# A decoder layer on one core: a new order of the steady slot on all engines

## The chip, the cores and the metric

The kernel runs on one core of a Trainium2 chip. The metric is the device time of one execution in microseconds (us). Five engines work side by side: PE (TensorE, matrix products and transposes), DVE (VectorE), ACT (ScalarE), POOL (GpSimd) and SP (SyncE, which issues most of the transfers). Each engine works through its own list of instructions in order, and they wait for each other by semaphores.

## The reference

The inputs are 16 sequences of 128 tokens with 256 features, and a context of the same shape. All arithmetic is in float32. Cut to what matters:

```python
x = x + self_attention(layernorm(x))                  # 16 heads of 64, no mask
x = x + cross_attention(layernorm(x), context, mask)  # 16 heads of 16, masked keys
x = x + experts(layernorm(x))                         # 8 experts of 512, all are evaluated

# experts: top-1 gate g -> norm_g = g / (g + 1e-6)
h = gelu(einsum('nd,edh->neh', xf, w1) + b1)
y = einsum('neh,ehd->ned', h, w2) + b2
out = (y * norm_g[:, None, None]).sum(axis=1)
```

Because the gate's factor does not depend on the expert, the experts can be summed before they are scaled. The change does not touch the expert stage.

## The kernel before

**Slots.** The two attentions run as a software pipeline of 16 slots, one for each sequence. Slot s does the self attention of sequence s, the first half of the cross attention of sequence s - 1 (queries, scores, softmax) and the second half of the cross attention of sequence s - 2 (transposed probabilities, values, output). It also does the key, query and value projections of two coming sequences at a time, by a Strassen-like scheme of seven products in place of eight. Slots 2 to 13 have nearly the same content and are called steady here. After slot 15 comes a short drain, and then the experts (from about 500 us on).

**The order is a table.** Every step of a slot is pushed on a heap by `at(name, f)` with a due time: slot s starts at `EXTRA + s * SLOT`, and `DUE[name]` is added. `run_slots` then pops all steps in order of these times and emits their instructions. PE, DVE, ACT and POOL are scheduled manually, so this order is the order of each engine's list. `FIRST_DUE` and `SECOND_DUE` hold exceptions for slots 0 and 1. A due time above `SLOT` reaches into the next slot. The due times set the order alone: what starts when is decided on the chip by the semaphores.

**The steps that matter here**, by the names in the table:

- `S0`, `S1`: self scores of one half of the heads each (`self_scores`, L693). `max0`, `max1`: largest score (L394, DVE). `ex0a` to `ex1b`: four exponentials each (L400, ACT). `r0a` to `r1b`: reciprocals of the sums (L411, DVE). `mul0a` to `mul1b`: normalization (L415, POOL). `T1a1` to `T1b2`: four transposes each (L430, PE), evacuated from PSUM by `T1a1e` to `T1b2e` on ACT.
- The same with a `c` or as `T2...` for the cross attention: `CQ` queries (L806), `q2T` their evacuation on DVE, `CS` scores (L828), `msk0`, `msk1` the mask, `cmax`, `cex`, `cr`, `cmul`, then `T2a1` to `T2b2`, of which `T2a1e`, `T2a2e` run on ACT and `T2b1e`, `T2b2e` on DVE.
- `SVa`, `SVb`: self values (L718), evacuated by `atT0`, `atT1` on DVE. `CV`: cross values (L867), `at2T`. `SO`, `CO`: output projections (L738, L887), added to the tokens by `xsSO`, `xsCO`.
- `cvr`: cross value rows (L782, `cross_value_rows`), evacuated by `cvre` on ACT. `ck`: cross keys (L755, `cross_keys`), evacuated by `cke`, `cke2` on ACT.
- `bn`, `bn3`, `root`, `xn`, `xn3`: statistics, inverse root (12 small DVE instructions) and normalization. `ab1`, `ab2`: a bias added to the tokens on POOL (L383). `LNx`, `LN1`, `LN3`: transposes of normalized tokens (L379), evacuated by `LNxc`, `LN1c`, `LN3c` on ACT.
- The paired projections: `v1x`, `v1y`, `v2x`, `v2y` for values (L643), and the same with q and k for queries and keys (L552). The first step opens one PSUM tile with the halves a and b, the second one with f and e; the third adds to a, the fourth to f and e. `vu0` to `vu3`, `vc00`, `vc1`, `vc0` read the halves out (and the same with q and k): `u1` reads b, `c00` reads a for the last time, `c1` and `c0` read f and e for the last time.

**Narrow steps.** The score and value products use a part of the array: `S0`, `S1` in row tiles of 64, `CS` in row tiles of 32, `CV` in column tiles of 32, `SVa`, `SVb` in column tiles of 64. All others use the whole array.

**PSUM.** The scores have a pool of two tiles of two banks each. All other outputs of PE share `ps_mm`, four tiles of one bank each:

```python
ps_mm = both.enter_context(
    tc.tile_pool(name="ps_mm", bufs=4, space=bass.MemoryType.PSUM, side="right")
)
```

**Transfers.** The context of two sequences is one load, double buffered; the load for the group after next is issued by SP behind the last use of the present one. In slots 14 and 15 the first two quarters of `w1` are loaded (`load_w1`, at `S0`), and `pre_hidden` starts on expert products at the places that the projections leave free (`PRE_STEPS`).

Of the kernel before, what the change touches and what calls it, by code (L numbers as in the profile page):

```python
# [30 lines left out]
GB = 2  # L31
NG = B // GB
# [17 lines left out]
NROW = 528  # L50


SLOT = 26.98
EXTRA = 7.86
DUE = dict(
    S0=0.0, S1=1.0, T2a1=2.05, T2a2=2.49, T2a1e=2.69, ck=2.92, T2a2e=3.19, max0=3.47, v1x=3.79,
    cke=3.99, vu0=4.3, cke2=4.4, max1=4.61, v1y=4.66, q1x=5.52, ex0a=5.54, vu1=6.08, q1y=6.42,
    vu2=6.76, qu0=6.91, vu3=7.24, r0a=7.32, v2x=7.32, mul0a=7.39, vc00=7.4, ex0b=7.41, qu1=7.63,
    v2y=7.77, qu2=8.06, qu3=8.49, LNx=8.6, q2x=8.64, vc1=8.84, q2y=9.09, LNxc=9.1, ex1a=9.13,
    vc0=9.19, r0b=9.53, mul0b=9.81, qc1=10.19, cvr=10.21, qc00=10.51, qc0=10.54, r1a=10.98,  # L60
    T2b1=11.23, mul1a=11.26, cvre=11.31, ex1b=11.66, T2b2=11.66, T2b1e=11.86, CQ=12.1,
    T2b2e=12.46, T1a1=12.97, q2T=13.17, T1a2=13.4, r1b=13.51, xn1=13.6, T1a1e=13.6, mul1b=13.79,
    CS=13.93, st0=14.0, mid=14.0, late=14.0, T1a2e=14.1, ab1=14.9, CV=14.97, msk0=15.08,
    LN3=16.07, at2T=16.27, T1b1=16.29, LN3c=16.49, msk1=16.61, T1b2=16.73, T1b1e=16.93,
    LN1=17.16, T1b2e=17.43, SVa=17.47, cmax0=17.8, LN1c=17.93, SVb=18.38, tf=18.93, mid2=18.93,
    atT0=18.94, late2=18.94, cex0a=19.12, k1x=19.43, atT1=19.54, cmax1=20.14, k1y=20.33,
    cex0b=20.49, SO=21.23, cr0a=21.28, cmul0a=21.56, ku0=21.86, cr0b=22.14, cex1a=22.36,
    cmul0b=22.58, ku1=22.58, ku2=23.01, ku3=23.44, cex1b=23.74, cr1a=23.94, st1=24.0,
    cmul1a=24.3, k2x=24.68, xsSO=24.88, k2y=25.12, bn=25.28, kc00=25.32, cr1b=25.78, CO=26.03,
    cmul1b=26.06, kc1=26.22, kc0=26.57, xsCO=27.09, bn3=27.5, root=28.09, xn=34.27, ab2=34.3,  # L70
    xn3=37.78,
)


FIRST_DUE = dict(
    fk0=-11.4, fq0=-9.5, fk0e=-9.4, fq0e=-7.7, fk1=-7.2, norm1=-7.0, S0=-5.4, fk1e=-5.3,
    fq1=-4.4, max0=-4.0, cross=-3.0, ex0a=-2.7, fLN=-2.65, fq1e=-2.6, fv0=-2.3, fLNc=-1.4,
    r0a=-1.32, ex0b=-1.3, mul0a=-1.2, S1=-0.6, fv0e=0.1, r0b=0.15, mul0b=0.2, fab0=0.25,
    fab1=0.3, max1=0.4, fv1=0.41, ex1a=1.65, early0=1.7, early1=1.75, cvr=2.22, fv1e=3.0,
    r1a=3.1, mul1a=3.2, early2=3.3, early3=3.35, ex1b=3.6, q0=3.96, cvre=5.0, r1b=5.1,  # L80
    mul1b=5.2, q0e=5.3, early=5.4, k0=6.57, ke0=8.56, ws0=8.7, v0=9.18, xn1=10.44, T1a1=10.9,
    ve0=11.1, T1a2=11.34, T1a1e=11.54, T1b1=11.77, T1a2e=12.14, T1b2=12.21, LN1=12.64,
    T1b1e=12.74, LN1c=13.06, T1b2e=13.34, w0q=13.6, w0k=13.7, SVa=14.25, SVb=15.15, atT0=15.42,
    q1=17.2, atT1=17.21, wv0=17.3, q1e=17.6, k1=18.0, w1q=18.1, tf=18.2, SO=19.16, ke1=19.6,
    ws1=19.7, w1k=20.0, xsSO=22.81, bn=23.22, v1=23.47, root=24.79, xn=25.0, ck=25.2, ve1=25.39,
    q1x=26.9, cke=26.9, cke2=26.91, qu0=26.95, q1y=27.8, qu1=28.2, ab2=28.44, ab1=28.5,
    k1x=28.7, qu2=28.8, k1y=28.9, qu3=29.2, ku0=29.3, ku1=29.85, ku2=30.0, ku3=30.1, q2x=30.5,
    q2y=30.95, qc00=31.0, qc1=32.0, qc0=32.5, k2x=32.8, kc00=33.3, k2y=33.4, kc1=34.5, kc0=34.9,
# [15 lines left out]
def decoder_layer(  # L104
# [53 lines left out]
    def psum_mm(name):  # L158
        return ps_mm.tile([P, 512], F32, tag="mm", name=name)
# [51 lines left out]
    def context(g):  # L211
        c = work.tile([P, KD, GT], F32, tag="ctx", name=f"ctx{g}")
        nc.sync.dma_start(out=c, in_=ctxT[g])
        return c

    contexts = {0: context(0)}
# [55 lines left out]
    def urgent():  # L272

        return tc.high_priority()
# [5 lines left out]
    def at(name, f, *a):  # L280


        if now[0] is None:
            f(*a)
        else:
            heapq.heappush(events, (when(name), next(count), now[0], f, a))

    def due(name, f, *a):

        if now[0] is None:  # L290
            with urgent():
                f(*a)
        else:
            at(name, f, *a)

    def when(name):
# [3 lines left out]
        if s == 1 and name in SECOND_DUE:  # L300
            return EXTRA + SLOT + SECOND_DUE[name]
        return EXTRA + s * SLOT + DUE[name]

# [445 lines left out]
    def cross_keys(b):  # L749
        kT = work.tile([P, C2, 2, T], F32, tag="k2T", name="k2T")  # L750
        g, i = b // GB, b % GB
        mm = psum_mm("mm_k2")[:, : C2 * T].rearrange("p (m t) -> p m t", m=C2)
        for m in range(C2):
            for k in range(KD):
                nc.tensor.matmul(  # L755
                    mm[:, m, :],
                    wx[:, 1, k, m * P : (m + 1) * P],
                    contexts[g][:, k, i * T : (i + 1) * T],
                    start=(k == 0),
                    stop=(k == KD - 1),  # L760
                )


        def out(m):
            for e in range(2):
                nc.scalar.activation(
                    kT[:, m, e, :],
                    mm[:, m, :],
                    AF.Identity,
                    bias=bkp[:, e, m : m + 1],  # L770
                    scale=par[:, e : e + 1],
                )

        due("cke", out, 0)
        due("cke2", out, 1)
        entry["k2T", b] = kT

    def cross_value_rows(b):
        g, i = b // GB, b % GB
        mm = psum_mm("mm_v2")  # L780
        for k in range(KD):
            nc.tensor.matmul(  # L782
                mm[:, :D],
                contexts[g][:, k, i * T : (i + 1) * T],
                wx_vo[:, 0, k, :],
                start=(k == 0),
                stop=(k == KD - 1),
            )
        due(
            "cvre",  # L790
            nc.scalar.copy,
            v2s[g % 2][:, i].rearrange("p (e w) -> p e w", e=2)[:, :, :D].rearrange(
                "p e (r t) -> p e r t", t=32
            )[:, :, :, :DH2],
            mm[:, :D].rearrange("p (r e d) -> p e r d", e=2, d=DH2),
        )
        if i == GB - 1 and g + 2 < NG:
            contexts[g + 2] = context(g + 2)

    def cross_queries(b):  # L800
        xnT2 = entry.pop(("xnT2", b))
# [210 lines left out]
    def slot(s):  # L1012


        for half in range(2):
            at(f"S{half}", self_scores, s, half)
            at(f"SV{'ab'[half]}", self_values, s, half)
            for n in range(2):
                at(f"T1{'ab'[half]}{n + 1}", self_transposed, s, half, n)
                if s >= 2:  # L1020
                    at(f"T2{'ab'[half]}{n + 1}", cross_transposed, s - 2, half, n)
        at("SO", self_output, s)
        at("cvr", cross_value_rows, s)
        at("ck", cross_keys, s)
        normalize_outputs(s, s - 2 if s >= 2 else None)
        if s >= 1:
            at("LNx", cross_norm, s - 1)
            at("CQ", cross_queries, s - 1)
            at("CS", cross_scores, s - 1)
            at("CS", cross_softmax, s - 1)  # L1030
        if s >= 2:
            at("CV", cross_values, s - 2)
            at("CO", cross_output, s - 2)
        if s >= 3:
            at("LN3", expert_norm, s - 3)
        bs = [2, 3] if s == 0 else [s + 3, s + 4] if s % 2 and s + 4 < B else []
# [3 lines left out]
        if bs:  # L1040
            at("LN1", self_norm_transposed, bs)
        b0 = s + 2 - s % 2
# [18 lines left out]
        if s >= B - 2:  # L1061
            at("S0", load_w1, s - (B - 2), we1)
        for n, (s1, name, out) in enumerate(PRE_STEPS):
# [459 lines left out]
```

## Time and profile before

| | |
|---|---|
| median of 3 runs | 858.39 us (858.09 to 858.63) |
| the profiled execution | 858.56 us |
| its span | 856.8 us |
| PE busy | 846.4 us (99%) |
| PE weight loads busy | 721.0 us (84%) |
| DVE busy | 642.6 us (75%) |
| ACT busy | 473.7 us (55%) |
| POOL busy | 164.1 us (19%) |
| granted TensorE clock | 0.999 |

The busy time of an engine is the union of its instructions' times. PE's instructions overlap: each starts before the one ahead of it has ended, so small stops do not show in the busy share but in the distance between starts. In the timeline rows of the profile the columns are the start in us, the length in us, engine, line, operation, output and inputs, the tile of the array and the shape, and the count of instructions merged into the row. In the rows of waits the columns are total us, times and longest us.

### The profile page before, as it was taken

To read this page: it belongs to the slowest core of one execution; us is meant where nothing else is said; L and a number is where in the kernel's file an instruction comes from. 1 tells how busy PE (TensorE), PEld (TensorE's weight loads), DVE (VectorE), ACT (ScalarE), POOL (GpSimd) and SP (SyncE) were. 2 spreads that over 40 slices of the span, in tenths; PEclk is the share of its full clock that TensorE was granted. 3 is DMA by queue.
4 is the path that set the end of the run, shared out by engine and by line. 5 is a ranking of instruction groups with operands and counts; after the bars stand their busy time and mean duration, and the time that the engine had idled before them with its cause. 6 is when DMAs were issued, how large, how long until landed. Compare 5 with 4: busy or idle time off the path is not lost.

```text
span 856.8 us, 16387 instructions
## 1 busy us (share of the span) xinstructions
PE 846.4 (99%) x5934; PEld 721.0 (84%) x5934; DVE 642.6 (75%) x1697; ACT 473.7 (55%) x1720; POOL 164.1 (19%) x179
## 2 busy tenths in 40 slices
PE   9999999999999999999999999999999999999997
PEld 7899889898898988898765458888888888888886
DVE  5888998989888888888657497776566756576655
ACT  3567677776877768686774523343434343343332
POOL 5133242432424334232341000000000000000000
PEclk9999999999999999999999999999999999999999
DMA  8500000000000000001240100000000000000000
GB/s 238 148 14 2 2 15 1 14 1 2 14 1 14 2 2 14 2 1 50 93 170 34 50 1 0 1 13 13 1 0 1 26 1 0 1 13 13 2 0 26
DMA packets 18321, 21.32 MB, mean 25 GB/s; under 512 B 9584, under 2 KB 13696, under 8 KB 17600
## 3 DMA queue, kind: packets, MB, share of 16 engines
q1 hardware_dynamic: 17728, 19.93, 7.4%
q8 instruction: 47, 0.77, 0.4%
q0 software_dynamic: 368, 0.30, 0.2%
q14 instruction: 34, 0.28, 0.1%
q10 hardware_dynamic: 144, 0.04, 0.0%
HBM read 18.16 MB, written 2.10 MB: 24 GB/s over the span
## 4 chain that ended last, share of the span: by engine, by line
PE 90%; DVE 6%; ACT 2%; issue 1%; DMA 1%; DVEq 0%; SPq 0%
PE y L1264 19%; PE mm_qk L552 10%; PE mm_o L738 6%; PE tr_p L430 6%; PE he L1264 5%; PE hf L1264 5%; PE ha L1264 5%; PE mm_v L643 5%; PE sc L693 4%; PE po L718 3%; PE mm_h L1002 3%; PE hb L1264 3%; PE po L867 2%; PE sc L828 2%; PE mm_qk L487 2%; PE mm_k L755 2%
## 5 line engine op out<-in xcount | busy, mean ns | idle before, releaser
L400 ACT ACTIVATE cpr<-sc,nmax 128x128 f32<-128x128 f32 x256 | 90.5, 403 | 17.7 <-DVE nmax L394 14.1
L400 ACT ACTIVATE pr<-sc,nmax 128x128 f32<-128x128 f32 x256 | 92.8, 408 | 2.6 <-DVE nmax L394 2.6
L415 POOL TENSOR_TENSOR cpr<-cpr,rinv 128x512 f32<-128x512 f32 x64 | 65.5, 1039 | 126.2 <-DVE rinv L411 126.0
L1293 ACT ACTIVATE h<-u,colv 128x256 f32<-128x256 f32 x56 | 28.4, 508 | 95.0 <-DVE u L1280 93.2
L415 POOL TENSOR_TENSOR pr<-pr,rinv 128x512 f32<-128x512 f32 x64 | 67.1, 1049 | 57.5 <-DVE rinv L411 54.5
L394 DVE TENSOR_REDUCE nmax<-sc 128x8 f32<-128x1024 f32 x64 | 76.4, 1214 | 0.2 <-PE sc L693 0.2
L1294 DVE TENSOR_TENSOR c<-u,hf 128x256 f32<-128x256 f32 x56 | 23.5, 420 | 68.2 <-PE hf L1264 68.0
L1277 ACT COPY u<-ha 128x256 f32<-128x256 f32 x56 | 20.8, 372 | 84.0 <-PE ha L1264 84.0
L1264 PE MATMUL hf<-xt,w 128*128 128x256 f32 x224 | 66.8, 380 | 0.4 <-DVE u L1279 0.4
L1264 PE MATMUL ha<-xnT,w 128*128 128x256 f32 x224 | 66.6, 379 | 0.0
L1264 PE MATMUL y<-t,w 128*128 128x256 f32 x224 | 66.6, 380 | 0.0
L400 ACT ACTIVATION_READ_ACCUMULATOR pr<-sc,nmax 128x1 f32 x256 | 63.4, 248 | 0.0
L400 ACT ACTIVATION_READ_ACCUMULATOR cpr<-sc,nmax 128x1 f32 x256 | 62.1, 243 | 0.0
L738 PE MATMUL mm_o<-wo,atT 128*128 128x256 f32 x256 | 58.1, 380 | 0.3 <-DVE atT L312 0.3
L1264 PE MATMUL y<-h,w 128*128 128x256 f32 x224 | 57.6, 379 | 0.0
L738 PEld LDWEIGHTS mm_o<-wo,atT 128*128 128x128 f32 x256 | 47.6, 190 | 7.4 <-issue 1.0
L1264 PEld LDWEIGHTS ha<-xnT,w 128*128 128x128 f32 x224 | 42.6, 190 | 7.1 <-issue 1.2
L1264 PEld LDWEIGHTS hf<-xt,w 128*128 128x128 f32 x224 | 42.4, 190 | 6.7 <-DVE u L1279 1.0
L1264 PEld LDWEIGHTS y<-h,w 128*128 128x128 f32 x224 | 42.6, 190 | 5.8
L1264 PEld LDWEIGHTS y<-t,w 128*128 128x128 f32 x224 | 41.9, 190 | 6.2 <-issue 0.8
L383 POOL TENSOR_TENSOR xs<-xs,rowv 128x256 f32<-128x256 f32 x32 | 23.3, 739 | 121.5 <-DVE xn L370 121.5
L312 DVE COPY_PREDICATED_SCALAR sc<-hidden_keys,masked 128x1024 f32 x30 | 38.4, 1279 | 8.6 <-PE sc L828 8.6
(251 smaller groups left out, 2074.0 us busy)
## 6 DMA issues: line engine op xcount, KB each, us to landing
w<-in_w SPq DMA_DIRECT2D x8, 1024.0 KB, 5.2
ctx<-in_ctxT SPq DMA_DIRECT2D x8, 256.0 KB, 2.6
out_x<-ot SPq DMA_DIRECT2D x8, 256.0 KB, 2.1
xs<-in_x SPq DMA_DIRECT2D x3, 512.0 KB, 5.5
wk<-in_wk SPq DMA_DIRECT2D x2, 512.0 KB, 7.3
wq<-in_wq SPq DMA_DIRECT2D x2, 512.0 KB, 7.9
wv<-in_wv SPq DMA_DIRECT2D x2, 512.0 KB, 10.0
wo<-in_wo SPq DMA_DIRECT2D x1, 1024.0 KB, 7.4
```

The source lines that it names most:

```text
L312: f(*a)
L394: nc.vector.tensor_reduce(w["nmax"], sc, AX.X, ALU.max, negate=True)
L400: nc.scalar.activation(w["pr"][:, i, :], sc[:, i, :], AF.Exp, bias=w["nmax"][:, i : i + 1], scale=1.0, accum_out=sums[:, j : j + 1],)
L415: nc.gpsimd.tensor_tensor(four, four, w["rinv", n].unsqueeze(2).broadcast_to([P, 4, T]), ALU.mult)
L430: nc.tensor.transpose(tr[:, j, :], w["pr"][:, 4 * n + j, :], ident)
L552: nc.tensor.matmul(out[:, q, :], paired[x, n][m - 1][:, q], paired[b0][m - 1], start=clears and q == 0, stop=True, skip_group_check=True,)
L643: nc.tensor.matmul(out, paired[b0][m - 1], paired["v", n][m - 1], start=clears, stop=True, skip_group_check=True,)
L693: nc.tensor.matmul(sc[:, j, c * T : (c + 1) * T], qT[r, c, :], kT[r, c, :], start=True, stop=True,)
L718: nc.tensor.matmul(po[j * DH1 : (j + 1) * DH1, c, :], v[:, h * DH1 : (h + 1) * DH1], prT[:, 4 * j + c, :], start=True, stop=True,)
L738: nc.tensor.matmul(mm[:, :D], atT[:, c, :], wo[:, c, :], start=(c == 0), stop=(c == C1 - 1))
L1264: nc.tensor.matmul(out, left[p // q][n - 1][:, p % q], rights[n - 1], **flags)
L1293: nc.scalar.activation(h[:, 1, 1], u[:, 3], AF.Gelu, bias=col(B1 + 2 * p + 1))
```

## The change

The table of due times is replaced, so the steps of the steady slots come in a new order on PE, DVE, ACT and POOL. On PE, `CV`, `SVa` and `SVb` follow `CS` directly (before, transposes stood between `CV` and `SVa`), `CO` follows `SVb` instead of standing ahead of `S0`, `ck` stands between `SO` and `k2x` near the slot's end instead of behind `T2a`, `LNx` stands behind `q2x`, and `T2b1`, `T2b2` come ahead of `cvr`. On DVE, `max0` comes ahead of the 12 instructions of `root`, `max1` behind `qu3`, both cross maxima behind `atT0` and `atT1`, and `vc1` and `qc1` behind `q2T`. On ACT, `T2a` and the cross keys are evacuated at other places, and the eight exponentials `ex1a`, `ex1b` stand together ahead of `cvre`. On POOL, `cmul1a` comes behind `ab2`. The load of the context moves with the last step that reads it, from `cvr` to `ck`. The exceptions for slots 0 and 1 and the expert stage stay as they are.

```diff
-SLOT = 26.98
+SLOT = 26.86
 EXTRA = 7.86
 DUE = dict(
-    S0=0.0, S1=1.0, T2a1=2.05, T2a2=2.49, T2a1e=2.69, ck=2.92, T2a2e=3.19, max0=3.47, v1x=3.79,
-    cke=3.99, vu0=4.3, cke2=4.4, max1=4.61, v1y=4.66, q1x=5.52, ex0a=5.54, vu1=6.08, q1y=6.42,
-    vu2=6.76, qu0=6.91, vu3=7.24, r0a=7.32, v2x=7.32, mul0a=7.39, vc00=7.4, ex0b=7.41, qu1=7.63,
-    v2y=7.77, qu2=8.06, qu3=8.49, LNx=8.6, q2x=8.64, vc1=8.84, q2y=9.09, LNxc=9.1, ex1a=9.13,
-    vc0=9.19, r0b=9.53, mul0b=9.81, qc1=10.19, cvr=10.21, qc00=10.51, qc0=10.54, r1a=10.98,
-    T2b1=11.23, mul1a=11.26, cvre=11.31, ex1b=11.66, T2b2=11.66, T2b1e=11.86, CQ=12.1,
-    T2b2e=12.46, T1a1=12.97, q2T=13.17, T1a2=13.4, r1b=13.51, xn1=13.6, T1a1e=13.6, mul1b=13.79,
-    CS=13.93, st0=14.0, mid=14.0, late=14.0, T1a2e=14.1, ab1=14.9, CV=14.97, msk0=15.08,
-    LN3=16.07, at2T=16.27, T1b1=16.29, LN3c=16.49, msk1=16.61, T1b2=16.73, T1b1e=16.93,
-    LN1=17.16, T1b2e=17.43, SVa=17.47, cmax0=17.8, LN1c=17.93, SVb=18.38, tf=18.93, mid2=18.93,
...
-    cmul1a=24.3, k2x=24.68, xsSO=24.88, k2y=25.12, bn=25.28, kc00=25.32, cr1b=25.78, CO=26.03,
-    cmul1b=26.06, kc1=26.22, kc0=26.57, xsCO=27.09, bn3=27.5, root=28.09, xn=34.27, ab2=34.3,
-    xn3=37.78,
+    S0=0.0, S1=1.06, max0=1.2, T2a1=2.11, ex0a=2.52, T2a2=2.54, v1x=2.98, v1y=3.84, T2a2e=3.89,
+    vu0=4.39, q1x=4.71, T2a1e=4.74, vu1=5.11, r0a=5.46, vu2=5.59, q1y=5.61, qu0=5.81,
+    mul0a=5.89, vu3=6.02, ex0b=6.31, v2x=6.51, qu1=6.53, v2y=6.94, qu2=6.96, qu3=7.39,
+    vc00=7.68, max1=7.74, q2x=7.81, LNx=8.4, qc00=8.46, q2y=8.62, r0b=8.88, LNxc=8.96, xn1=9.01,
+    mul0b=9.16, ex1a=9.26, vc0=9.34, T2b1=9.52, qc0=9.72, T2b2=9.95, T2b1e=10.16, ab1=10.18,
+    cvr=10.39, ex1b=10.63, r1a=10.83, T2b2e=10.96, mul1a=11.11, T1a1=11.26, CQ=11.69, cvre=12.0,
+    r1b=12.2, T1a1e=12.35, mul1b=12.48, LN3=12.56, q2T=12.76, T1a2=12.78, LN3c=12.98, vc1=13.1,
+    LN1=13.22, T1b1=13.44, qc1=13.45, LN1c=13.64, T1b2=13.87, T1a2e=13.94, tf=14.16, CS=14.4,
+    T1b2e=14.51, st0=14.56, mid=14.56, late=14.56, st1=14.57, T1b1e=15.01, CV=15.45, msk0=15.55,
+    SVa=16.49, at2T=16.74, msk1=17.08, SVb=17.39, mid2=18.3, late2=18.3, atT0=18.4, CO=18.44,
...
+    cex0b=23.75, ck=24.55, xsSO=24.75, ku3=25.09, cex1b=25.12, k2x=25.42, cr0b=25.44,
+    cr1a=25.57, bn=25.7, cmul0b=25.72, k2y=25.87, kc00=26.5, kc1=26.97, cke=27.0, cke2=27.05,
+    kc0=27.32, cr1b=27.76, cmul1b=28.04, root=29.2, xn=31.55, ab2=32.05, cmul1a=33.77,
+    xn3=38.42,
 )
...
         due("cke", out, 0)
         due("cke2", out, 1)
+        if i == GB - 1 and g + 2 < NG:
+            contexts[g + 2] = context(g + 2)
         entry["k2T", b] = kT
...
-        if i == GB - 1 and g + 2 < NG:
-            contexts[g + 2] = context(g + 2)
```

More of the change, by code (lines that the diff above doesn't have):

```diff
@@ L50 @@
 NROW = 528
-SLOT = 26.98
+SLOT = 26.86
 EXTRA = 7.86
 DUE = dict(
-    S0=0.0, S1=1.0, T2a1=2.05, T2a2=2.49, T2a1e=2.69, ck=2.92, T2a2e=3.19, max0=3.47, v1x=3.79,
-    cke=3.99, vu0=4.3, cke2=4.4, max1=4.61, v1y=4.66, q1x=5.52, ex0a=5.54, vu1=6.08, q1y=6.42,
-    vu2=6.76, qu0=6.91, vu3=7.24, r0a=7.32, v2x=7.32, mul0a=7.39, vc00=7.4, ex0b=7.41, qu1=7.63,
-    v2y=7.77, qu2=8.06, qu3=8.49, LNx=8.6, q2x=8.64, vc1=8.84, q2y=9.09, LNxc=9.1, ex1a=9.13,
-    vc0=9.19, r0b=9.53, mul0b=9.81, qc1=10.19, cvr=10.21, qc00=10.51, qc0=10.54, r1a=10.98,
-    T2b1=11.23, mul1a=11.26, cvre=11.31, ex1b=11.66, T2b2=11.66, T2b1e=11.86, CQ=12.1,
-    T2b2e=12.46, T1a1=12.97, q2T=13.17, T1a2=13.4, r1b=13.51, xn1=13.6, T1a1e=13.6, mul1b=13.79,
-    CS=13.93, st0=14.0, mid=14.0, late=14.0, T1a2e=14.1, ab1=14.9, CV=14.97, msk0=15.08,
-    LN3=16.07, at2T=16.27, T1b1=16.29, LN3c=16.49, msk1=16.61, T1b2=16.73, T1b1e=16.93,
-    LN1=17.16, T1b2e=17.43, SVa=17.47, cmax0=17.8, LN1c=17.93, SVb=18.38, tf=18.93, mid2=18.93,
-    atT0=18.94, late2=18.94, cex0a=19.12, k1x=19.43, atT1=19.54, cmax1=20.14, k1y=20.33,
-    cex0b=20.49, SO=21.23, cr0a=21.28, cmul0a=21.56, ku0=21.86, cr0b=22.14, cex1a=22.36,
-    cmul0b=22.58, ku1=22.58, ku2=23.01, ku3=23.44, cex1b=23.74, cr1a=23.94, st1=24.0,
-    cmul1a=24.3, k2x=24.68, xsSO=24.88, k2y=25.12, bn=25.28, kc00=25.32, cr1b=25.78, CO=26.03,
-    cmul1b=26.06, kc1=26.22, kc0=26.57, xsCO=27.09, bn3=27.5, root=28.09, xn=34.27, ab2=34.3,
-    xn3=37.78,
@@ new lines @@
+    r1b=12.2, T1a1e=12.35, mul1b=12.48, LN3=12.56, q2T=12.76, T1a2=12.78, LN3c=12.98, vc1=13.1,
+    LN1=13.22, T1b1=13.44, qc1=13.45, LN1c=13.64, T1b2=13.87, T1a2e=13.94, tf=14.16, CS=14.4,
+    T1b2e=14.51, st0=14.56, mid=14.56, late=14.56, st1=14.57, T1b1e=15.01, CV=15.45, msk0=15.55,
+    SVa=16.49, at2T=16.74, msk1=17.08, SVb=17.39, mid2=18.3, late2=18.3, atT0=18.4, CO=18.44,
+    atT1=18.5, k1x=19.3, cmax0=19.69, k1y=20.2, ku0=20.4, cmax1=20.83, cex0a=21.01, SO=21.1,
+    xsCO=21.97, cex1a=22.38, cr0a=22.58, bn3=22.71, cmul0a=22.86, ku1=23.21, ku2=23.64,
```

## The prediction

> **What bounds the kernel now.** Three views, in this order. First the page's busy line and the waits of PE:
>
> ```profile
> PE 846.4 (99%) x5934; PEld 721.0 (84%) x5934; DVE 642.6 (75%) x1697; ACT 473.7 (55%) x1720; POOL 164.1 (19%) x179
> ...
> PE mm_qk L487 <- DMA wk<-in_wk: 0.8, 1, 0.8
> PE tr_p L430 <- ACT v L312: 0.6, 1, 0.6
> PE po L867 <- DVE cprT L292: 0.5, 2, 0.3
> ```
>
> PE never stops and is never seen to wait over 1.1 us: whatever lengthens the PE chain lengthens the kernel. But matmul ends lie about 0.16 us behind the next start, so a gap under that is counted as busy. It shows only in start-to-start times, so I read the PE timeline of one steady slot (S0 of it at 235.78, of the next at 262.66: 26.88 us; slots with LN1, four more transposes, take 27.32):
>
> ```profile
> 235.78 2.06 PE L693 MATMUL sc<-kT,qT 64*128 64x128 f32 x32
> 237.76 1.09 PE L430 MATMUL tr_p<-ident,cpr 128*128 128x128 f32 x8
> 238.69 1.06 PE L755 MATMUL mm_k<-ctx,wx 128*128 128x128 f32 x8
> 239.59 0.60 PE L643 MATMUL mm_v<-wv,xnT 128*128 128x256 f32 x2
> ...
> 243.96 0.59 PE L643 MATMUL mm_v<-sums_v,xnT 128*128 128x256 f32 x2
> 244.40 0.38 PE L379 MATMUL tr_x<-ident,xn 128*128 128x128 f32 x2
> 244.61 0.61 PE L552 MATMUL mm_qk<-xnT,wq 128*128 128x128 f32 x4
> 245.18 0.71 PE L552 MATMUL mm_qk<-sums_v,wq 128*128 128x128 f32 x4
> 245.73 0.61 PE L552 MATMUL mm_qk<-xnT,sums_q 128*128 128x128 f32 x4
> 246.18 1.03 PE L782 MATMUL mm_v<-wx_vo,ctx 128*128 128x256 f32 x4
> 247.04 1.05 PE L430 MATMUL tr_p<-ident,cpr 128*128 128x128 f32 x8
> 247.93 1.06 PE L806 MATMUL mm_q<-xnT,wx 128*128 128x128 f32 x8
> 248.82 1.04 PE L430 MATMUL tr_p<-ident,pr 128*128 128x128 f32 x8
> 249.79 1.15 PE L828 MATMUL sc<-k2T,q2T 32*128 32x256 f32 x16
> ```
>
> Four 128-wide matmuls take 0.445 us, yet q2x takes 0.57 and the first half of q2y 0.55: q2y waited 0.12 and, its weight loads no longer running ahead, lost 0.10 more. The DVE timeline names the cause, and shows what an evacuation costs:
>
> ```profile
> 244.71 0.42 DVE L312 TENSOR_TENSOR qT<-su,mm_qk 128x256 f32<-128x256 f32 x1
> ...
> 247.24 0.40 DVE L370 TENSOR_SCALAR xn<-xs,mv,root 128x256 f32<-128x256 f32 x1
> 247.56 0.17 DVE L411 RECIPROCAL rinv<-sums 128x4 f32<-128x4 f32 x1
> 247.68 1.29 DVE L312 COPY cprT<-tr_p 128x512 f32<-128x512 f32 x2
> 249.03 0.42 DVE L312 TENSOR_TENSOR q2T<-mm_q,bqk 128x256 f32<-128x256 f32 x1
> ```
>
> qu3 ends at 245.13 and q2y starts at 245.18: DVE's end to PE's start is 0.05. The other way is 0.04 (mm_q's last matmul starts at 248.71 and ends 0.28 later; q2T starts at 249.03).
>
> **The change part by part.** Nothing is added or removed: the DUE times reorder the same instructions on PE, DVE, ACT and POOL.
>
> *Gains on PE.* (a) LNx goes between q2x and q2y and qu3 comes earlier, so the 0.22 above goes. (b) CS, CV, SVa, SVb stand side by side. In single records of the trace, going from CV to the transposes costs 0.11 on the first start-to-start and 0.06 on the second, going from transposes to SV 0.09 and 0.05: together 0.31. They become one CV-to-SV passage that the trace does not show; bounds are nothing and a full entry plus exit, 0.31. I take CS to CV (0.11 + 0.02), the only row between two narrow forms: gain 0.18. [...]
>
> *What it costs: the four mm banks.* In the slots all PE outputs but the scores use ps_mm, 4 PSUM banks; a step that finds none free stops PE, and every step queued behind it on PE waits too. A paired step holds two: a/b, and f/e until its last reader. Those readers move: vc1 from 8.84 to 13.10 and qc1 from 10.19 to 13.45, behind q2T on DVE. So v's and q's f/e banks stay taken, and T2b1, T2b2, cvr, T1a1, CQ, LN3, T1a2 share two. In the compiled program T2b1, cvr, CQ and T1a2 use one bank, T2b2, T1a1, LN3 the other; each waits for its predecessor's evacuation. The table's times (T2b1e 10.16, cvr 10.39) leave no room for a copy of 0.69.
>
> Now the walk, in us after S0, in a slot without LN1. PE steps by the rows: S0 and S1 1.98, T2a 0.93, v1x and v1y 1.72, q1x and q1y 1.79, v2x and v2y 1.30, q2x 0.45, LNx 0.21, q2y 0.89: T2b1 starts at 9.27, T2b2 at 9.71, and cvr could start at 10.16. DVE in the compiled program's new order: max0 1.20 (half of the 1.98, and 0.2 to the last matmul's end), root 2.33 (12 small instructions, 2.37), xn 4.70, vu1, r0a, vu2, vu3, qu1 to qu3 (rows: 0.33, 1.0, 0.5, 1.3) to 7.8, max1 1.13, r0b, vc0 to 9.4, qc0 (needs q2y's end, 9.48) to 10.00.
> - cvr waits for T2b1e: 10.01 + 0.68 + 0.05 = 10.74, a wait of 0.58. With DVE free at once T2b1 still ends at 9.88, so the wait is at least 0.50.
> - CQ waits for cvre: with a restart of 0.10, cvr's last matmul ends at 11.87; ACT has just done eight exponentials (11.86) and copies until 12.36 (0.45); CQ starts at 12.41, where PE was ready at 12.15: 0.26.
> - T1a2 waits for q2T: CQ (0.99) and LN3 (0.22) pass PE by 13.62; CQ's end 13.57, q2T 13.60 to 14.03, T1a2 at 14.08: 0.46.
>
> Each wait also costs the restart seen at q2y (0.10, 0.10; 0.03 before transposes). Sum 1.30 + 0.23 - 0.22 - 0.18 = +1.13, in slots 4, 6, 8, 10, 12, 13. In slots 3, 5, 7, 9, 11 the two xn1 normalizations (0.33 each start to start) stand on DVE ahead of vc0, T2b1e starts at 10.52 and cvr waits 1.09: +1.64. Together 6 x 1.13 + 5 x 1.64 = 15.0. Later stages have slack: the sc banks are free for S0 about 1.8 us early, cmul1a passes POOL about 1.3 us before T2b1, PE's wait for the two atT is covered by CO and k1x.
>
> *Edges.* Slot 1: eight exponentials (0.34 each) stand in one block ahead of cvre, CQ waits 1.8; k2y waits 1.2 for ku3, on DVE behind both cross maxima (1.13 each); 0.4 at smaller places; less gains and the 0.7 that slot 1 already loses: +2.5. Slot 2: like slot 4 plus 0.7 at k2x, less its own present 0.33: +1.3. Slot 14: w1_0's load is issued by k2y's end, now just after S0, and takes 5.2 (page, w<-in_w); it lands at 5.5, but q1x's pre_hidden is reached at 4.65 (5.54 before): 0.9, then 0.2, 0.65 and 0.1 for banks, 0.4 for S0 behind the late cross exponentials: +2.4 with restarts. Slot 15 and exit: POOL's queue now has ab2 before cmul1a; at the end no next slot covers that. SO, xsSO, bn, root (2.4), xn 0.41, ab2 0.73, cmul1a 1.04 end at 31.3 after S0, PE reaches T2b1 at 27.3: 4.1. Slot 15's other waits hardly change: +3.8.
>
> *Hidden.* ck moves by most of a slot to before k2x: same 0.90 of PE, and its evacuation has until CS, 14 us later. The ctx loads (2.6 us) go out a third of a slot later but are read a slot after that. max0 ahead of root delays xn to 5.1 and LNx is at 8.2; max1 comes after qu3 and ex1a only needs to end before T1b1. If PE's own waits were gone, the next in line would be T1b1 and T1b2, whose probabilities leave POOL about 1.9 us ahead of them.
>
> Sum: 15.0 + 2.5 + 1.3 + 2.4 + 3.8 = 25.0. The profiled execution took 858.56 (span 856.8 and 1.8 around it, which nothing here touches), 0.17 over the median of the runs; its rows carry the sum, so 858.56 + 25.0 = 883.6 for it and 883.4 for a median run.
>
> [...]
>
> **The rivals.**
> 1. Faster: the bank waits do not bind and only gains are left, 13 x 0.40 = 5.2: 853. That decides if T2b1's copy ended by 10.1. Against it: T2b1 itself ends at 9.88. Chance 0.03. That the reorder does nothing (858.4) has 0.01.
> 2. Milder: waits absorb each other, q2T and cvre come earlier, exit stalls are covered by pre_hidden work: the core 15.0 falls to 11, edges 10 to 5: 874. For: PE order near the exit has ready work, though the queue is fixed. Chance 0.11.
> 3. Worse: every wait shifts ACT's exponentials too, S0 and S1 then wait 0.4 for the score banks in each slot, as in slot 15: 13 x 0.5 more, 890. Against: 1.8 us of slack. Chance 0.10.
> The forecast above: 0.75.
>
> **How the numbers follow.** The likeliest case is 883.4. Sizes unknown: CV-to-SV (-1.7 to +2.3), slots 1 and 14 to exit (10 us, good to about 4), semaphore delays. The range takes in rival 3 and the upper edge of rival 2: 875 to 891. A measurement of this kernel can tell about 0.2% from no change. Faster 0.03, same 0.01, slower 0.96.
>
> **What would show it.** Steady slots of 28.0 and 29.0 us in S0 starts; PE waits of L784 for DVE cprT (0.5 to 1.1 us), of L806 for ACT (0.3), of L430 for DVE q2T (0.5), a dozen times each, and busy share of PE down to about 96%; q2x to q2y without the 0.22; one wait of L1002 for a w load; one tr_p wait near 4 us for POOL. Slots under 26.9 and no cvr wait would prove me wrong.

## The result and the profile after

The changed kernel takes 889.82 us (median of 5 runs, 889.41 to 890.88), the kernel before 858.39 us beside it (5 runs, 858.09 to 858.95): 1.037 times as long, 95% interval 1.035 to 1.038. The span of the profiled execution grew from 856.8 to 888.0 us, by 31.2. The page's busy line (engine, busy us, share of the span, instructions):

```profile
PE 851.9 (96%) x5934; PEld 723.3 (81%) x5934; DVE 641.1 (72%) x1697; ACT 473.8 (53%) x1720; POOL 164.3 (19%) x179
```

PE's busy time grew by 5.5 us only; the other 26 us are gaps, and here many are long enough to be seen. The waits of PE (who waits for whom: us in total, times, longest):

```profile
PE mm_v L784 <- DVE cprT L312: 10.9, 12, 1.6
PE tr_p L430 <- POOL cpr L415: 6.1, 2, 5.0
PE tr_p L430 <- DVE q2T L312: 4.5, 12, 0.4
PE mm_q L806 <- ACT v L312: 1.6, 1, 1.6
PE mm_qk L552 <- DVE kT L312: 1.0, 1, 1.0
```

The first and the third come once in each of the slots 2 to 13: `cvr` waits for `T2b1e`, `T1a2` for `q2T`. The fourth and fifth are slot 1; the second is the exit (5.0) and slot 15 (1.1). PE's timeline shows where they stand in slot 8 (its `S0` at 247.59), and, in the last two rows, what is different in slot 9:

```profile
255.34 0.61 PE L552 MATMUL mm_qk<-xnT,wq 128*128 128x128 f32 x4
255.78 0.40 PE L379 MATMUL tr_x<-ident,xn 128*128 128x128 f32 x2
256.02 0.61 PE L552 MATMUL mm_qk<-sums_v,wq 128*128 128x128 f32 x4
...
256.92 1.04 PE L430 MATMUL tr_p<-ident,cpr 128*128 128x128 f32 x8
258.38 1.13 PE L784 MATMUL mm_v<-wx_vo,ctx 128*128 128x256 f32 x4 [0.42 <-DVE cprT L312]
259.35 0.60 PE L430 MATMUL tr_p<-ident,pr 128*128 128x128 f32 x4
260.00 1.16 PE L806 MATMUL mm_q<-xnT,wx 128*128 128x128 f32 x8
261.00 0.38 PE L379 MATMUL tr_x<-ident,xn 128*128 128x128 f32 x2
261.77 1.50 PE L430 MATMUL tr_p<-ident,pr 128*128 128x128 f32 x12 [0.39 <-DVE q2T L312]
...
264.27 1.08 PE L867 MATMUL po<-cprT,v 128*32 128x128 f32 x32
265.28 1.09 PE L718 MATMUL po<-prT,xnT 128*64 128x128 f32 x16
...
285.04 1.04 PE L430 MATMUL tr_p<-ident,cpr 128*128 128x128 f32 x8
287.66 1.13 PE L784 MATMUL mm_v<-wx_vo,ctx 128*128 128x256 f32 x4 [1.58 <-DVE cprT L312]
```

Read it by starts; a bracket at the end of a row is the idle time that the profile saw before it, and what ended it. `q2x`, `LNx`, `q2y` follow at 0.44 and 0.24: the stop that was there is gone. The eight transposes of `T2b` (0.87 without a wait) hold PE for 1.46, `T1a1` (0.44) for 0.65, `LN3` (0.24) for 0.77: three waits of 0.59, 0.21 and 0.53, of which the bracket shows only the part beyond the busy tail (for the second, nothing). In slot 9 the first of them is 1.75.

From `S0` to the next `S0`, us:

| stage | before | after | measured | predicted |
|---|---|---|---|---|
| slot 1 | 24.38 | 27.06 | +2.68 | +2.5 |
| slot 2 | 27.21 | 27.88 | +0.67 | +1.3 |
| slots 4, 6, 8, 10, 12, 13 | 26.88 (6: 27.24) | 28.12 | +7.1 in all | +6.8 |
| slots 3, 5, 7, 9, 11 | 27.32 (3, 5: 27.44) | 29.69 | +11.6 in all | +8.2 |
| slot 14 | 25.54 | 28.20 | +2.66 | +2.4 |
| slot 15 to the experts | 77.87 | 84.85 | +7.0 | +3.8 |
| start to slot 1 | 47.87 | 47.32 | -0.5 | 0 |

The last row is the start up to the first `S0`, which lies between 12.6 and 13.3 us in all profiles of this study, and slot 0, which is the same.

### The profile page after: what moved, and what is told of

Its sections match the earlier page's. It is cut to its first block, busy times and chain, and to the rows that moved or that the text cites. A ratio compares the mean times of both kernels' runs of the same rounds, so it can differ in the third digit from the quotient of the medians.

```text
span 888.0 us, 16349 instructions
## 1 busy us (share of the span) xinstructions
PE 851.9 (96%) x5934; PEld 723.3 (81%) x5934; DVE 641.1 (72%) x1697; ACT 473.8 (53%) x1720; POOL 164.3 (19%) x179
## 4 chain that ended last, share of the span: by engine, by line
PE 79%; DVE 10%; ACT 6%; issue 3%; DMA 1%; POOL 0%; DVEq 0%; ACTq 0%
PE y L1264 18%; PE mm_qk L552 6%; PE he L1264 5%; PE hf L1264 5%; PE mm_o L738 5%; PE ha L1264 5%; PE tr_p L430 5%; PE sc L693 3%; PE po L718 3%; PE mm_h L1002 3%; ACT pr L400 3%; PE mm_v L643 3%; PE hb L1264 3%; PE mm_q L806 2%; PE sc L828 2%
## 5 line engine op out<-in xcount | busy, mean ns | idle before, releaser
L400 ACT ACTIVATE pr<-sc,nmax 128x128 f32<-128x128 f32 x256 | 90.9, 387 | 14.1 <-DVE var L358 7.7
L400 ACT ACTIVATION_READ_ACCUMULATOR cpr<-sc,nmax 128x1 f32 x256 | 64.7, 253 | 0.0
L400 ACT ACTIVATION_READ_ACCUMULATOR pr<-sc,nmax 128x1 f32 x256 | 57.8, 226 | 0.0
L312 DVE COPY_PREDICATED_SCALAR sc<-hidden_keys,masked 128x1024 f32 x30 | 38.4, 1279 | 18.7 <-PE sc L828 18.7
L563 ACT ACTIVATE su<-mm_qk,bk 128x128 f32<-128x128 f32 x28 | 8.8, 364 | 61.4 <-PE mm_qk L552 61.4
```

The costliest lines, as they stand in the source:

```text
L400: nc.scalar.activation(w["pr"][:, i, :], sc[:, i, :], AF.Exp, bias=w["nmax"][:, i : i + 1], scale=1.0, accum_out=sums[:, j : j + 1],)
```

## The experiments

The diffs show the changed entries of the table alone, and the ratios are to runs of the kernel before made beside each experiment.

Theory A is the prediction's: the late `vc1` and `qc1` keep two of the four mm banks, and the steps from `T2b1` to `T1a2` wait on the other two. Rival B: the narrow steps side by side cost the time. Rival C: the order on DVE around `max0`, `root` and `max1` does. Theory D came with the first traces: a POOL multiplication holds up a DVE instruction beside it (in the changed kernel one `xn` alone takes 0.41 us, and the two of `xn1` beside a multiplication took 1.43 together).

**1. The changed kernel with vc1 and qc1 early.**

```diff
-vc1=13.1, qc1=13.45
+vc1=9.33, qc1=9.71
```

> The changed kernel, with vc1 and qc1 (the reads that release the f/e banks of the v and q projections) put directly ahead of vc0 and qc0 again. Theory A (too few PSUM banks for T2b1 to T1a2): the waits of cvr, CQ and T1a2 go from the even slots, which fall from 28.13 to about 26.5 us; odd slots keep 0.3 to 0.5 at cvr because the two xn1 normalizations still stand ahead of T2b1e on DVE, 27.5; slot 1 loses its CQ wait, the exit keeps its 5 us. In all 871 us (868 to 874). Rival B (the four narrow steps side by side are what costs): steady slots stay above 28, 888 or more. Rival C (DVE order around max0, root, max1 is what costs): the same instructions stand in DVE's list, steady slots fall by less than 0.5, 883 or more.

Measured: 876.63 us, 1.020 of before (1.019 to 1.022). Even slots took 26.99 us, odd slots 28.75, slot 1 26.42. Undoing this one move takes 13.2 of the 31.4 us away, and the even slots, with the narrow steps side by side and the new DVE order still in them, are back within 0.11 of before: for the even slots A holds, and B and C, which left them above 28 or nearly unchanged, fall. For the other 18 us this says nothing, and 871 was expected. PE's timeline of slot 8 names the new wait:

```profile
252.42 1.06 PE L806 MATMUL mm_q<-xnT,wx 128*128 128x128 f32 x8
253.68 0.41 PE L379 MATMUL tr_x<-ident,xn 128*128 128x128 f32 x2 [0.21 <-DVE rinv L411]
```

`CQ` (0.89) and 0.37 of waiting: `LN3` is next in line, late because `xn3` comes late on DVE and takes 0.86 there instead of 0.41 (experiment 4 shows why). So a part of C is left: the place of a step on DVE costs here too, if far less. The odd slots keep over a microsecond that is not a matter of banks.

**2. The kernel before with vc1 and qc1 late.**

```diff
-vc1=8.84, qc1=10.19
+vc1=13.3, qc1=13.45
```

> The kernel before, with vc1 and qc1 alone put behind q2T on DVE, as the change has them. Theory A: this one move takes two of the four mm banks from the middle of the slot; steady slots grow by 1.1 to 1.7 us, in all 875 us (872 to 880). Rivals B and C (narrow steps side by side, DVE order): this move alone is worth under 3 us, 861 or less.

Measured: 881.19 us, 1.026 (1.024 to 1.027); even slots 28.67, 1.79 more than before. The same move alone, in the old order, costs 22 us, more than the 13.6 to 21.6 that were expected. The waits stand at other steps (`T2b1` 0.63 for `qc00` on ACT, `CQ` 0.35 for `T2b1e`), which fits a shortage of banks: the wait falls on the step that asks next, wherever that is in the order.

**3. The changed kernel with xn1 behind T2b2e.** `ab1` then adds its bias ahead of `xn1`, so the odd slots normalize other numbers; the work is the same.

```diff
-xn1=9.01
+xn1=12.0
```

> The changed kernel, with xn1 (two normalizations on DVE, in odd slots) put behind T2b2e. Theory A with the mis-sized xn1 pair (1.43 us instead of 0.66): cvr's wait in odd slots falls from 1.58 to the 0.42 of even slots, 5 slots of 1.1 us, about 884 us, even slots unchanged at 28.13. If later readers on DVE (q2T, LN1) take the delay instead, a part comes back: 886 to 888. Rival: odd slots are long for the four more LN1 transposes and their bank waits alone, then nothing moves: 889.8.

Measured: 884.01 us, 1.029 (1.028 to 1.031). Odd slots 28.56, even ones 28.12: what is left between them is the 0.44 of `LN1`. So the excess of the odd slots over the even ones, 5 x 1.13 beside `LN1`, was `xn1` ahead of `T2b1e`.

**4. The changed kernel with xn1 where POOL is idle.**

```diff
-xn1=9.01
+xn1=7.6
```

> The changed kernel, with xn1 ahead of max1 on DVE, where POOL has nothing to do, and still ahead of ab1. Theory D (a normalization on DVE and a POOL multiplication exclude each other): the pair takes about 0.75 us instead of 1.43, cvr's wait in odd slots falls from 1.58 to about 0.9, odd slots from 29.69 to about 29.0; 5 x 0.7 = 3.5 less, 886.3; some of slot 1 may give back 0.6. Rival (the pair is slow by itself, 0.7 each): the pair still takes 1.43 and the time stays at 889.8.

Measured: 887.70 us, 1.034 (1.032 to 1.035). Odd slots 29.13 instead of 29.69, `cvr`'s longest wait there 0.9 instead of 1.6; slot 1 became 0.6 longer and the exit 0.7, so 887.7 came and not the 886.3 expected. The row to see is the pair of normalizations, in slot 9 of this kernel (DVE's timeline):

```profile
282.60 0.73 DVE L370 TENSOR_SCALAR xn<-xs,mv,root 128x256 f32<-128x256 f32 x2
```

and the same two instructions in slot 9 of the changed kernel, with POOL's row beside them:

```profile
284.73 1.43 DVE L370 TENSOR_SCALAR xn<-xs,mv,root 128x256 f32<-128x256 f32 x2
```

```profile
284.89 1.12 POOL L415 TENSOR_TENSOR pr<-pr,rinv 128x512 f32<-128x512 f32 x1 [1.25 <-DVE rinv L411]
```

POOL ends at 286.01 and the second `xn` at 286.16: it ended only when POOL was done. The pair is not slow by itself.

**5. The changed kernel with cmul1a ahead of ab2, in all slots.**

```diff
-cmul1a=33.77
+cmul1a=32.0
```

> The changed kernel, with cmul1a ahead of ab2 in POOL's list. Theory A: at the end the last sequence's cmul1a no longer stands behind SO, bn, root, xn and ab2; PE's 4.97 us wait falls to about 2 us, and because PE then idles less the granted clock does not fall to 0.50 for the 5 us behind it: 3 us of wait and 2 us of clock, 884.7. Rival D1 (the wait is real, but the lower clock hides no time): 3 us only, 886.8. Rival D2 (the wait only moves to T2b2 or the last po): 889. Steady slots unchanged in all.

Measured: 893.78 us, 1.040 (1.038 to 1.042), a miss. The exit became shorter by 3.0 us as expected, but the slots 3 to 13 grew by 0.62 to 0.70 each. DVE's timeline of slot 8 and POOL's:

```profile
253.66 0.99 DVE L358 TENSOR_SCALAR var<-mv 128x2 f32<-128x2 f32 x1
```

```profile
252.59 2.04 POOL L415 TENSOR_TENSOR cpr<-cpr,rinv 128x512 f32<-128x512 f32 x2 [1.44 <-PE sc L693]
```

Two elements a partition take 0.16 us in the changed kernel; here 0.99, and they end at 254.65 where POOL's two multiplications end at 254.63. `root`, `xn` and the evacuations next behind them on DVE are 0.7 to 0.8 us later. Two elements are next to nothing to move, and the 0.83 us more end where POOL's work does: that fits an instruction that is held up until POOL has ended better than one that runs more slowly beside it. By what means POOL holds it up no trace here shows. In the traces of the two kernels only `TENSOR_SCALAR` rows of DVE grow beside a POOL multiplication (in the changed kernel `xn` from 0.41 to 0.87 at the median, `var` of four elements from 0.16 to 0.65); evacuations from PSUM (`su` 0.42 and 0.42), the reductions of the scores (1.22 and 1.22) and reciprocals (0.17 and 0.18) grow by 0.01 us at most. The exit of this experiment adds a `TENSOR_TENSOR` that reads `root` alone, 0.95 us where it takes 0.16 without POOL, which also ends where POOL's multiplication does (484.7):

```profile
483.77 0.95 DVE L335 TENSOR_TENSOR root_t<-root 128x2 f32<-128x2 f32 x1
```

And not every `TENSOR_SCALAR` is held: in slot 2 of the kernel before, two of one element a partition (`var`, `root_t`) ran in 0.14 and 0.15 us in the midst of a POOL multiplication (73.02 to 74.06).

**6. The same in the last slot alone.**

```diff
+EDGE = {1: SECOND_DUE, B - 1: dict(cmul1a=27.9)}
...
-        if s == 1 and name in SECOND_DUE:
-            return EXTRA + SLOT + SECOND_DUE[name]
+        if name in EDGE.get(s, ()):
+            return EXTRA + s * SLOT + EDGE[s][name]
```

> The changed kernel, with cmul1a ahead of ab2 on POOL in the last slot alone. Theory A, as the run that moved it in all slots suggests: steady slots as in the changed kernel (28.12 and 29.69), PE's exit wait 4.97 falls to about 1.8, 889.8 - 3.0 = 886.8; a lower clock still follows the wait. Theory D: with cmul1a first in all slots, the 0.6 us that every steady slot got longer came from cmul1a on POOL holding up DVE's first root instruction (0.99 us instead of 0.16), so they are back to 28.12 here. Rival: that growth came from something else in the order at the end, then slots stay at 28.7 and 30.4 and the time at 893.

Measured: 885.33 us, 1.031 (1.030 to 1.033). Steady slots 28.12 and 29.69 as in the changed kernel, so experiment 5's growth was `cmul1a` on POOL beside DVE. The exit is 4.9 us shorter than in the changed kernel, not 3.0. Its waits come to 1.9 us instead of 5.2; the rest, some 1.6 to 1.9 by this estimate (each stop also has up to 0.16 that the brackets do not show), goes with TensorE's clock. The exit in the changed kernel, PE's timeline, and its windows of 5 us (the figures behind the engines' busy times are the granted clock, DMA share, GB/s):

```profile
474.37 1.04 PE L430 MATMUL tr_p<-ident,cpr 128*128 128x128 f32 x8
480.38 1.97 PE L430 MATMUL tr_p<-ident,cpr 128*128 128x128 f32 x8 [4.97 <-POOL cpr L415]
```

```profile
475.00:480.00 5.00, 0.41 (x4) 0.17 (x2) 3.33 (x14) 2.56 (x7) 2.54 (x3) 0.86 0.19 80
480.00:485.00 5.00, 4.41 (x41) 3.13 (x41) 1.38 (x2) 0.00 (x0) 0.33 (x1) 0.50 0.01 3
```

and the windows with the same work in this experiment:

```profile
475.00:480.00 5.00, 3.12 (x30) 1.92 (x32) 4.45 (x14) 2.99 (x9) 2.13 (x3) 1.00 0.28 118
480.00:485.00 5.00, 5.00 (x47) 3.63 (x40) 2.28 (x7) 1.24 (x3) 0.83 (x1) 1.00 0.01 3
```

The clock falls to 0.50 some 3 us into the wait of 5 and stays there for 6.8 us, 5.1 of them with work, and the same eight transposes take 1.97 instead of 1.04. In this experiment the waits are 0.34, 0.34, 1.01 and 0.19 us and the clock stays at 1.00.

**7. The changed kernel with all four repairs** (`vc1`, `qc1` as in 1, `xn1` as in 4, `cmul1a` as in 6, and `xn3` ahead of `r1a`):

```diff
-xn1=9.01, vc1=13.1, qc1=13.45, xn3=38.42
+xn1=7.6, vc1=9.33, qc1=9.71, xn3=37.5
...
+EDGE = {1: SECOND_DUE, B - 1: dict(cmul1a=27.9)}
```

> The changed kernel with vc1 and qc1 early, xn1 ahead of max1, xn3 ahead of r1a (both where POOL is idle), and cmul1a ahead of ab2 in the last slot. If banks, POOL and exit add up: even slots 26.8 to 26.9 (LN3 no longer waits), odd slots 27.7 to 27.9, exit as in the run that moved cmul1a in the last slot alone: 868 us (865 to 871). The rest over the kernel before would then be in slots 1 and 14 (2 us each), odd slots (0.5 each) and the exit (4 us). Rival: the pieces overlap, and the sum is not reached: 872 or more.

Measured: 868.79 us, 1.012 (1.010 to 1.014): the pieces add up. But the even slots stayed at 26.96. `LN3` no longer waits, and the twelve transposes behind it hold PE for 1.76 instead of the 1.45 of experiment 1: the wait moved on to the next step instead of going. What is left over the kernel before, 9.1 us in the profiled execution, lies in slots 1 (2.0) and 14 (2.2), the five odd slots (2.9) and slot 15 with the exit (2.1).

**8. The changed kernel's order, worked over** (23 due times moved, 13 more in slots 1, 14 and 15, and the first expert product of slot 14 put behind its load). In the core:

```diff
-T1a1=11.26, CQ=11.69, r1b=12.2, mul1b=12.48, LN3=12.56, CS=14.4, CV=15.45, cmul1b=28.04
+T1a1=11.44, CQ=11.34, r1b=11.2, mul1b=13.68, LN3=13.36, CS=15.2, CV=14.41, cmul1b=31.71
```

with `vc1=7.72`, `qc1=9.48`, `xn1=8.56` and smaller moves; `CV` now precedes `CS`.

> The changed kernel's PE order with the waits taken out: vc1 and qc1 ahead of vc0 and qc0, xn1 and the other normalizations where POOL is idle, CQ ahead of T1a1, CV and CS exchanged with T1b so that fewer stand behind one bank, the first weight product of slot 14 moved behind the load, and cmul1a ahead of cmul1b in the last slot. Theory A (the new PE order by itself is worth 0.2 to 0.6 us a slot, its waits cost the 31 us): even slots about 26.2 instead of 26.88, odd ones 27.1 to 27.3, slots 1, 14 and the exit still 0.5 to 2 us worse each: 857 us (854 to 860). Rival B (the order is bad in itself): even slots stay above 26.9, 862 or more.

Measured: 862.24 us, 1.005 (1.004 to 1.006), where 857 was expected. Even slots took 26.72 (slot 6: 27.43): 0.16 shorter than before, not 0.7. The profile's list of waits shows none in the steady slots but 2 and 6, so this is about what the PE order is worth as far as it got; in starts, both groups of eight transposes of `T1` still take 1.00 and 1.03, where eight take 0.87 without a stop. The odd slots (27.46 to 27.70), slots 1, 2 and 14 (0.9, 0.6 and 0.9) and the exit (2.7 us) take more than that back. Its exit has the waits of experiment 6 (0.34, 0.34, 1.01), yet its clock fell there:

```profile
455.00:460.00 5.00, 4.05 (x31) 2.40 (x32) 2.85 (x9) 0.00 (x0) 0.82 (x1) 0.66 0.01 3
```

**9. The kernel before with ten due times moved, and LN1 in slot 1.**

```diff
-vu0=4.3, T2b1=11.23, cvre=11.31, T2b1e=11.86, xn1=13.6, late=14.0, at2T=16.27, cmax0=17.8,
-mid2=18.93, late2=18.94
+vu0=5.3, T2b1=9.46, cvre=14.2, T2b1e=10.97, xn1=14.01, late=13.35, at2T=17.06, cmax0=16.99,
+mid2=20.69, late2=19.82
...
-SECOND_DUE = dict(wv1=4.7, st0=11.9, st1=12.46, st2=16.3, tf=19.6, st3=24.0)
+SECOND_DUE = dict(wv1=4.7, st0=11.9, st1=12.46, st2=16.3, tf=19.6, st3=24.0, LN1=18.24)
```

> The kernel before, with ten due times moved: T2b1 and T2b1e ahead of cvr (a bank comes free while cvr runs), cvre behind the four exponentials, xn1 behind q2T and the small late, late2, mid2, vu0 steps moved off the places where POOL multiplies or q2x waits; cmax0 and at2T exchanged; LN1 later in slot 1. Theory (waits under 0.3 us that the busy share hides are what is left in the kernel before): even slots from 26.88 to about 26.7, odd ones from 27.3 to 27.0, slots 1 and 2 0.3 to 1 shorter: 855 us (853 to 857). Rival (the order of before has no waits left to take): 858.4.

Measured: 855.08 us, 0.996 of before (0.995 to 0.997), as expected: faster than both kernels. Even slots 26.80, odd 27.23, slot 2 26.58 (27.21), slot 6 26.80 (27.24). `q2x` and `q2y` take 1.35 instead of 1.56, so the wait for `qu3` is gone without the new order; 0.10 comes back at `CQ`. In slots 2 and 6, 0.54 and 0.30 go at `k1y` and `SO`, which stood behind `mid2` and `late2` on DVE.

## Why the prediction was right, and where its sizes were off

The prediction said 883.4 us within 875 to 891, and 889.8 came: 31.4 us more than before, not 25.0. The direction and the main cause were right. That the number still lies inside the range is in part luck: the upper end was there for a rival (the third) that did not come, while the misses came at the odd slots and the exit. Point by point:

- **The bank shortage: right, shown from both sides** (experiments 1 and 2). In even slots the three waits were to be 0.58, 0.26 and 0.46 and measured 0.59, 0.21 and 0.53; two restarts of 0.10 are there. Sum +1.13 predicted, +1.24 measured. That a bank is what is waited for shows in the rows: `cvr` reads `wx_vo` and `ctx` and still waits for the copy into `cprT`, `T1a2` reads `pr` and waits for `q2T`.
- **The gains: right.** The 0.22 at `q2y` is gone. The passage from `CV` to `SVa` was priced at 0.13, between nothing and 0.31, for a gain of 0.18. In single records its starts are 0.203, 0.007 and 0.153 apart, as were those of the passage from transposes to `SVa` before. So one of two passages is saved, 0.10 and 0.05, some 0.15 in all.
- **The odd slots: the mechanism right, one term mis-sized.** "The two xn1 normalizations (0.33 each start to start)" took 1.43 us together, because one of them stands beside a POOL multiplication. `cvr` waited 1.75 us by starts instead of 1.09, and the five slots cost 11.6 instead of 8.2. The trace of before had shown it: its `xn1` pair also took 1.43 us beside a multiplication, in a place where PE did not wait for it (slot 9 of before, DVE and POOL):

```profile
276.44 1.43 DVE L370 TENSOR_SCALAR xn<-xs,mv,root 128x256 f32<-128x256 f32 x2
276.60 1.12 POOL L415 TENSOR_TENSOR pr<-pr,rinv 128x512 f32<-128x512 f32 x1 [0.78 <-DVE rinv L411]
```

The price of an instruction was taken from where it ran alone, and put where it did not.
- **Slot 15 and exit: +7.0 instead of +3.8, the largest miss.** The wait of 4.1 was 4.97, since POOL's multiplication held up `root` for 0.8 us (one instruction of `root` there took 0.94); the low clock added 1.6 to 1.9 (estimated at experiment 6), which no step of the sum had; and the waits inside slot 15, which were to change hardly, are 0.23 at `S1`, 1.10 at `T2b1` and 0.64 at `LN3`, 1.97 in all against 1.30 before (0.49, 0.60 and 0.21). The 0.54 at `S0` of slot 15 counts in slot 14, where the prediction had 0.4.
- **Slots 1, 2 and 14: right to 0.2, 0.6 and 0.3.** Slot 1 waits 1.6 for `cvre` and 1.0 for `ku3`, slot 14 0.6 for the `w1` load. In slot 2 the 0.7 expected at `k2x` is not there: from `ck` to the next `S0` its starts are those of slot 4.
- **The rivals.** The faster one fell with the first wait, the milder one with the sums (the core cost 18.7 and not 11, the edges 13.0 and not 5). Rival 3's time, 890, came, but not its mechanism: `S0` and `S1` waited in slot 15 only, not in each slot.

What is not settled: which of the small waits of slot 15 is due to which move, and what makes slots 1 and 14 longer move by move; these were not tried alone.

## What to carry over

Move a read and you move a tenant: a step that only evacuates PSUM decided here when a bank came free (13.2 us in experiment 1, 22 in experiment 2), and its price showed at other steps, whichever asked next. Before an instruction is priced by its mean, look whether it ran beside another engine in the place it comes from and the place it goes to (`xn` took 0.41 us alone and 0.87 beside a POOL multiplication). An order that hides a late engine by the next round's work has to be looked at once more in the last round, where there is none (here a wait of 4.97 us).

## What the hardware showed that was not expected

- DVE's `TENSOR_SCALAR` of two or more elements a partition, begun beside a running POOL multiplication of 128x512, was held up: 0.16 us became 0.99, 0.41 became 0.87, and the ones held to the end ended within 0.15 us of POOL's end. Two of one element were not held (0.14 and 0.15 us). The other way round the traces show little: a multiplication that began beside a running `xn` took 1.12 instead of 1.04.
- Waits of about 2 us of PE at the exit went with a lower clock in two runs and not in a third. In experiment 5 PE waited 1.79 and then 0.55, and right behind the second wait the clock was 0.50 for 3.4 us; the waits of experiments 6 and 8 are the same (0.34, 0.34, 1.01 and 0.19), and the clock stayed at 1.00 in one and fell to 0.66 over 5 us in the other; the 1.58 us waits of the odd slots in the changed kernel never lowered it. Executions of one kernel differ too: of the five of experiment 8, two took 863.5 and 864.1 us at a mean clock of 0.997, the others 862.1 to 862.2 at 0.998 to 0.999, and the trace shown is of one of the longer two. So the length of the longest wait alone does not decide it. The stretch at 0.50 around the exit lasted 6.8 us in the changed kernel and 3.4 in experiment 5; the mean clocks of the windows give some 6.9 for experiment 4 and 3.4 for experiment 8. What decides whether the clock falls no run here shows.
- Two evacuations of 0.4 us, moved behind `q2T`, were worth 13 us in one order (experiment 1) and 22 in the other (experiment 2).
